# The last column of every scan: copied by ScalarE instead of VectorE

## The chip, the cores and the metric

The kernel runs on one core of a Trainium2 chip. The metric is the device time of one execution in microseconds (us). A core has five engines that run their own instruction streams in order and meet at semaphores: TensorE (PE, with its weight loads shown as PEld), VectorE (DVE), ScalarE (ACT), GpSimd (POOL) and SyncE (SP), which here mostly issues DMA transfers. SBUF is the on-chip working memory and PSUM the memory that PE writes; DRAM tiles lie in the chip's large memory.

## The reference

Two layers on an input `x` of 8 images of 64 x 64 pixels and 96 channels. The first is a selective scan over the pixels in four directions, the second a small network between an upsampling and a downsampling; each stands on a group normalisation and is added to its input. What the change touches is the scan:

```python
def step(h, inp):
    ul, dl, Bl, Cl = inp
    dA = jnp.exp(dl[..., None] * A)
    h = dA * h + (dl * ul)[..., None] * Bl[:, :, None, :]
    y = jnp.einsum('bkdn,bkn->bkd', h, Cl)
    return (h, y)
_, ys = lax.scan(step, h0, (u_t, d_t, B_t, C_t))
...
x = x + _L0_conv_ref(_gn(x), ...)
x = x + _L1_conv_ref(_gn(x), ...)
```

There are 4 directions (`k`), 192 channels (`d`), 16 states (`n`) and 4096 pixels, so for each image and direction 192 x 16 = 3072 independent recurrences of 4096 steps.

## The kernel before

**Tiles.** The work is cut into 3072 tiles of 128 partitions by 1024 pixels. A tile holds 8 channels with their 16 states, so 24 tiles (`NT`) cover the channels of one stretch of 1024 pixels, called a chunk here; 4 chunks (`NCH`) make one direction of one image, 4 directions an image, 8 images the whole: 128 chunks. The order is image, direction, chunk, tile. Since a tile sees only a quarter of the pixels, the state at its end must be kept until the tile of the same channels in the next chunk, 24 tiles later. It is kept in one column of `carry`, an SBUF tile of 128 x 24 with one column for each of the 24 tiles. In the first chunk of a direction the scan starts from 0.0, and after the last chunk nothing is kept.

**The steps of a tile.** `fetch` (L1059) has SP load `dub`, each channel's row repeated for 16 states. `product_b` (L1067) has GpSimd multiply it by `br` into `bb`. `decay` (L1071) has PE spread the step sizes into the PSUM tile `pd` (four matmuls, L1075), and ScalarE takes the exponential in place (L1082). `scan` (L1084) has VectorE run the recurrence (L1089). `product_c` (L1093) multiplies the states by `cr` into `hc` (L1095). `hold` (L1104) copies the last column of the scan into `carry` (L1108). `sums` (L1118) has PE add up the states of two tiles at a time (L1127), and `store` (L1157) sends the result to DRAM by way of ScalarE and SP.

**Two kinds of tiles.** Every third tile is marked `by_pool` (L1054). For it the scan writes to the SBUF tile `h`, GpSimd does `product_c`, and ScalarE does `hold`. For the other two of three the scan writes back into `pd`, VectorE does `product_c` straight after the scan, and VectorE does `hold` straight after that. Here these are called GpSimd tiles and VectorE tiles.

**Buffers.** `pd` has two buffers of two PSUM banks, so the matmul of tile i+2 may only write when all readers of tile i are done: the scan alone for a GpSimd tile, and the scan, the product and the copy for a VectorE tile. `bb`, `dub` and `hc` have four buffers, `h` two.

**The order.** The loop at L1193 writes out the order by hand. In step i, each engine's stream receives: the fetch of tile i+6 on SP, the product of the GpSimd tile i-1 and then `product_b` of tile i+3 on GpSimd, `decay` of tile i+1 on PE and ScalarE, then `scan`, `product_c` and `hold` of tile i. After that `side.advance` (L1250) adds pieces of all other work: normalisation, convolution and gates of the next image, the preparation of the next chunk (`prepare`, L965), the layer norm and the second network of the image before. A planner, `Side`, gives them out with fixed allowances for each engine and step (`CAPS`, L49). Then come `turn_over`, which puts in a matmul whose result nobody reads (L1101) where PE has little side work, and `sums` for tiles i-3 and i-2. The order is fixed when the program is built and does not react to what happens on the chip.

So the stream of ScalarE in step i is: exponential of tile i+1; the copy of `hold` if tile i is a GpSimd tile; side work. The stream of VectorE is: scan of tile i; if it is a VectorE tile, product and copy; side work.

Of the kernel before, what the change touches and what calls it, by code (L numbers as in the profile page):

```python
# [136 lines left out]
def kernel(ctx: ExitStack, tc: tile.TileContext, a: dict, out: bass.AP):  # L137
    nc = tc.nc
# [965 lines left out]
    def hold(t):  # L1104
        if t["last"]:
            return
        end = T - 1 if t["k"] < 2 else 0
        (nc.scalar.copy if t["by_pool"] else nc.vector.tensor_copy)(  # L1108
            carry[:, t["g"] : t["g"] + 1], t["h"][:, end : end + 1]
        )  # L1110

# [60 lines left out]
    with tc.manual_schedule():  # L1172
# [20 lines left out]
        for i in range(n + 4):  # L1193
            t = tiles[i] if i < n else None
# [48 lines left out]
            if t:  # L1243
                scan(t)
                if not t["by_pool"]:
                    product_c(t)
                hold(t)
# [105 lines left out]
```

## Time and profile before

| what | value |
|---|---|
| median of 3 runs | 11125.21 us (11121.33 to 11125.94) |
| the profiled execution's own time | 11107.68 us |
| its span, first to last instruction | 11105.8 us |
| mean clock granted to TensorE | 0.982 |
| scans (L1089) on VectorE | 3072, 2280 to 2350 ns each by form |
| products on VectorE (L1095) | 2048, 1225 ns each |
| copies of `hold` on VectorE | 1536, 148 ns each |
| copies of `hold` on ScalarE | 768, 183 ns each |
| `product_b` on GpSimd (L1069) | 3072, 2359 ns each |
| products on GpSimd (L1095) | 1024, 2357 ns each |
| exponentials on ScalarE (L1082) | 3072, 1088 ns each |
| bytes moved by DMA | 2401.27 MB, mean 216 GB/s |

The counts follow from the tiling: 3072 x 2/3 = 2048 products on VectorE, and three chunks of four keep their state, so 2048 x 3/4 = 1536 copies on VectorE and 1024 x 3/4 = 768 on ScalarE.

How to read the profile lines: a group of instructions has its line in the kernel, engine, operation, output and inputs by the program's names, shapes and count; then the time in which the group kept its engine busy, the mean duration of one in ns, and the idle time of the engine just ahead of such instructions with what ended most of it (`<-`). In a timeline the columns are the start in us from the beginning of the span, the duration in us, the engine, the line, and the instruction; idle time before it stands in brackets. Two instructions that follow one another on an engine can overlap by a few hundredths of a us in the records. The releaser named is inferred from semaphores and can be a neighbour of the true one.

### The profile page before, as it was taken

How to read it: one execution, taken by the hardware profiler on the slowest of the kernel's cores; microseconds unless marked ns; L12 is line 12 of the kernel's file. 1: busy time of each engine (PE TensorE's matmuls, PEld its weight loads, DVE VectorE, ACT ScalarE, POOL GpSimd, SP SyncE). 2: the span in 40 equal slices, each digit the busy share in tenths (PEclk: the TensorE clock that was granted, in tenths of full speed). 3: DMA queues.
4: the chain of work that ended last, by engine and by line, in shares of the span. 5: the costliest groups of instructions: out<-in, count | busy, mean ns of one | idle time of the engine just before them, and what ended most of it. 6: DMA issues, size and time to landing. Idle time of an engine off the chain costs nothing. (4 is left out here: it accounts for less than half of the span.)

```text
span 11105.8 us, 137238 instructions
## 1 busy us (share of the span) xinstructions
PE 9967.9 (90%) x45020; PEld 3204.6 (29%) x45020; DVE 10207.5 (92%) x7702; ACT 5910.6 (53%) x8218; POOL 10179.6 (92%) x4674
## 2 busy tenths in 40 slices
PE   8898888989889998999889998899988989889988
PEld 2222222322233222332223322233222332223325
DVE  6999999999999999999999999999999999999990
ACT  5455445656455564555545555455554655545543
POOL 5999999999999999999999999999999999999990
PEclk9999999999999999999999999999999999999998
DMA  6888898898988989888988989889898898988981
GB/s 174 215 208 224 209 231 209 217 227 232 233 209 216 225 231 225 212 218 224 240 217 215 224 221 244 209 219 225 217 243 210 217 228 218 247 206 216 227 214 48
DMA packets 1044463, 2401.27 MB, mean 216 GB/s; under 512 B 293820, under 2 KB 314556, under 8 KB 1043752
## 3 DMA queue, kind: packets, MB, share of 16 engines
q1 hardware_dynamic: 1042776, 2391.45, 86.5%
q8 instruction: 361, 5.91, 0.2%
q14 instruction: 350, 2.87, 0.1%
q10 hardware_dynamic: 976, 1.04, 0.0%
HBM read 1929.05 MB, written 328.73 MB: 203 GB/s over the span
## 5 line engine op out<-in xcount | busy, mean ns | idle before, releaser
L1069 POOL TENSOR_TENSOR bb<-dub,br 128x1024 f32<-128x1024 f32 x3072 | 7173.5, 2359 | 208.4 <-DMA dub<-du 149.2
L1082 ACT ACTIVATE pd<-pd,neg_a 128x1024 f32<-128x1024 f32 x3072 | 3340.7, 1088 | 4533.0 <-PE pd L1075 4489.8
L1075 PE MATMUL pd<-dl,sel_b 64*128 64x512 f32 x12288 | 3512.7, 645 | 987.2 <-DVE carry L1108 649.2
L1089 DVE TENSOR_TENSOR_SCAN pd<-pd,carry,bb 128x1024 f32<-128x1024 f32 x1536 | 3610.3, 2350 | 262.2 <-ACT carry L1108 127.9
L1095 POOL TENSOR_TENSOR hc<-h,cr 128x1024 f32<-128x1024 f32 x1024 | 2413.9, 2357 | 352.6 <-DVE h L1089 300.7
L1095 DVE TENSOR_TENSOR hc<-pd,cr 128x1024 f32<-128x1024 f32 x2048 | 2508.4, 1225 | 164.1 <-PE py L1127 20.0
L1075 PEld LDWEIGHTS pd<-dl,sel_b 64*128 64x128 f32 x12288 | 966.7, 186 | 3266.3 <-issue 1511.2
L1089 DVE TENSOR_TENSOR_SCAN h<-pd,carry,bb 128x1024 f32<-128x1024 f32 x768 | 1797.3, 2340 | 5.8 <-ACT pd L1082 5.6
L1127 PE MATMUL py<-hc,sel_r 128*32 128x512 f32 x12288 | 1715.0, 617 | 30.4 <-POOL hc L1095 30.2
L1089 DVE TENSOR_TENSOR_SCAN pd<-pd,bb 128x1024 f32<-128x1024 f32 x512 | 1172.5, 2290 | 98.6 <-ACT carry L1108 75.3
L1101 PE MATMUL idle<-sel_b,ident 128*128 128x512 f32 x1652 | 932.0, 646 | 8.0 <-DVE ty L720 5.9
L562 PE MATMUL pc<-pad,convr 96*128 96x512 f32 (+1 forms) x2304 | 858.3, 616 | 5.7 <-DVE e L585 3.6
L1089 DVE TENSOR_TENSOR_SCAN h<-pd,bb 128x1024 f32<-128x1024 f32 x256 | 583.6, 2280 | 26.0 <-ACT pd L1082 25.2
L1127 PEld LDWEIGHTS py<-hc,sel_r 128*32 128x32 f32 x12288 | 250.3, 109 | 1109.0 <-issue 854.5
L1031 POOL TENSOR_TENSOR u<-dl,u 128x512 f32<-128x512 f32 x384 | 485.0, 1271 | 79.2 <-DVE dl L1028 79.2
L862 PEld LDWEIGHTS p<-w2q,mq 128*100 128x100 f32 x4800 | 452.9, 168 | 274.6 <-issue 214.2
L855 PE MATMUL ph<-xu,w 96*128 96x500 f32 x960 | 504.9, 629 | 11.5 <-ACT mq L856 6.7
L862 PE MATMUL p<-w2q,mq 128*100 128x96 f32 x4800 | 511.5, 258 | 2.3 <-ACT mq L856 2.3
L562 PEld LDWEIGHTS pc<-pad,convr 96*128 96x128 f32 (+1 forms) x2304 | 266.3, 163 | 563.9 <-issue 552.8
L987 PE MATMUL px<-u,xp 64*64 64x512 f32 x1536 | 422.4, 627 | 2.4 <-issue 2.4
L1101 PEld LDWEIGHTS idle<-sel_b,ident 128*128 128x128 f32 x1652 | 249.8, 189 | 596.5 <-issue 522.4
L1012 PE MATMUL pv<-xd,dt_w 64*64 64x512 f32 x1536 | 394.4, 609 | 1.0 <-ACT xd L997 1.0
(153 smaller groups left out, 6707.9 us busy)
## 6 DMA issues: line engine op xcount, KB each, us to landing
dub<-du SPq DMA_DIRECT2D x3072, 512.0 KB
u<-u SPq DMA_DIRECT2D x256, 384.0 KB
du<-u SPq DMA_DIRECT2D x768, 128.0 KB
y<-yq SPq DMA_DIRECT2D x768, 128.0 KB
br<-xd SPq DMA_DIRECT2D x256, 256.0 KB
cr<-xd SPq DMA_DIRECT2D x256, 256.0 KB
yp<-y SPq DMA_DIRECT2D x384, 128.0 KB
yp<-u SPq DMA_DIRECT2D x192, 128.0 KB
```

The lines of the kernel that those rows point to most:

```text
L562: nc.tensor.matmul(t[rows].rearrange("p (i j) -> p i j", i=8), weights[:, cs], v["pad"][:, 8 * blk + kw : 8 * blk + kw + 8, kh : kh + H], ...
L855: nc.tensor.matmul(t[:, :px], w1[:, m, :], xu, start=True, stop=True)
L862: nc.tensor.matmul(t[:SIDE, C * i : C * i + C], sq[:, m, row], w2q[:, m, :], start=(m == 0), stop=(m == 2))
L987: nc.tensor.matmul(p[rows], xp[rows, k, q, :], v["u"][rows, q, :], start=(q == 0), stop=(q == 2), skip_group_check=True,)
L1031: nc.gpsimd.tensor_tensor(v["u"][:, q, :], got["dl"][:, q, :], v["u"][:, q, :], ALU.mult)
L1069: nc.gpsimd.tensor_tensor(t["bb"], t["dub"], t["got"]["br"], ALU.mult)
L1075: nc.tensor.matmul(pd[:, MB * hf : MB * hf + MB], sel_b[rows, 4 * t["s"] + t["j"]].rearrange("p n c -> p (n c)"), t["got"]["dl"][rows, t[" ...
L1082: nc.scalar.activation(pd, pd, AF.Exp, scale=neg_a[:, t["k"], t["g"] : t["g"] + 1])
L1089: nc.vector.tensor_tensor_scan(t["h"][:, ::step], pd[:, ::step], t["bb"][:, ::step], 0.0 if t["first"] else held, ALU.mult, ALU.add)
L1095: (nc.gpsimd if t["by_pool"] else nc.vector).tensor_tensor(t["hc"], t["h"], t["got"]["cr"], ALU.mult)
L1101: nc.tensor.matmul(p, ident, sel_b[:, 0:4].rearrange("p j n c -> p (j n c)"), start=True, stop=True)
L1127: nc.tensor.matmul(py[r0 : r0 + 32], sel_r[:, t["j"], :], t["hc"][:, MB * hf : MB * hf + MB], start=(t["j"] == 0), stop=(t["j"] == 3 and t ...
```

## The change

`hold` no longer chooses its engine by the kind of tile: ScalarE makes the copy for every tile. The copy of a VectorE tile so moves from VectorE's stream, where it stood behind the product, to ScalarE's, where it stands behind the exponential of tile i+1 and ahead of the side work of step i; it reads one column of `pd` in PSUM and writes one column of `carry` in SBUF, as before. Nothing else is edited.

```diff
     def hold(t):
         if t["last"]:
             return
         end = T - 1 if t["k"] < 2 else 0
-        (nc.scalar.copy if t["by_pool"] else nc.vector.tensor_copy)(
+        nc.scalar.copy(
             carry[:, t["g"] : t["g"] + 1], t["h"][:, end : end + 1]
         )
```

## The prediction

> **What bounds the kernel now.** I read the head of the page first, then the groups by line, then the timeline around the copies, then the busy time of chosen stretches.
>
> ```profile
> span 11105.8 us, 137238 instructions
> PE 9967.9 (90%) x45020; PEld 3204.6 (29%) x45020; DVE 10207.5 (92%) x7702; ACT 5910.6 (53%) x8218; POOL 10179.6 (92%) x4674
> ...
> L1082 ACT ACTIVATE pd<-pd,neg_a 128x1024 f32<-128x1024 f32 x3072 | 3340.7, 1088 | 4533.0 <-PE pd L1075 4489.8
> L1075 PE MATMUL pd<-dl,sel_b 64*128 64x512 f32 x12288 | 3512.7, 645 | 987.2 <-DVE carry L1108 649.2
> L1089 DVE TENSOR_TENSOR_SCAN pd<-pd,carry,bb 128x1024 f32<-128x1024 f32 x1536 | 3610.3, 2350 | 262.2 <-ACT carry L1108 127.9
> ```
>
> VectorE and GpSimd are both 92% busy, ScalarE 53%: the copy leaves the fullest engine for the emptiest. The first scan starts at 120.1 us and the last ends at 10836.3, so 10716 us belong to the 3072 tiles, 3.49 us each, and little else can change. Counted over the records of that stretch, VectorE is idle about 560 us and GpSimd about 570: neither is the bound everywhere, and what one gains the other must follow. ScalarE's 4533 us of idle time lie before the exponentials, waiting for the matmul that fills `pd`.
>
> Two views of the copies themselves, both from the listing by line:
>
> ```profile
> L1108 DVE COPY carry<-pd x1536: 146/148/151, 123.6 to 10750.5; 128x1 f32<-128x1 f32 x192
> L1108 ACT COPY carry<-h x768: 172/182/193, 133.1 to 10754.4; 128x1 f32<-128x1 f32 x192
> ```
>
> **The part removed.** 1536 copies at 148 ns would be 227 us, but that is not what VectorE loses. The timeline of VectorE in image 0 shows the same two tiles in a chunk with copies and, one chunk on, in the last chunk of a direction, where the kernel makes none:
>
> ```profile
> 1279.64 1.23 DVE L1095 TENSOR_TENSOR hc<-pd,cr 128x1024 f32<-128x1024 f32 x1
> 1280.78 0.15 DVE L1108 COPY carry<-pd 128x1 f32<-128x1 f32 x1
> 1280.85 2.35 DVE L1089 TENSOR_TENSOR_SCAN pd<-pd,carry,bb 128x1024 f32<-128x1024 f32 x1
> ...
> 1360.01 1.23 DVE L1095 TENSOR_TENSOR hc<-pd,cr 128x1024 f32<-128x1024 f32 x1
> 1361.15 2.35 DVE L1089 TENSOR_TENSOR_SCAN pd<-pd,carry,bb 128x1024 f32<-128x1024 f32 x1
> ```
>
> From the product's start to the next scan's start it is 1.21 us with the copy and 1.14 without: neighbours on VectorE overlap, and a copy costs 0.065 us (the median distance from copy to scan over some 1290 pairs). 1536 x 0.065 = 100 us, the most that VectorE alone can give.
>
> How much of it arrives is shown by whole chunks, since every fourth chunk already runs without these copies. Three chunks of image 0 with the same work in the background, then one from the next direction of a later image (columns: stretch, length, busy time of PE, weight loads, DVE, ACT, POOL, clock, DMA share, GB/s):
>
> ```profile
> 1196.83:1277.19 80.36, 67.57 (x264) 17.30 (x260) 77.25 (x59) 34.24 (x46) 77.79 (x36) 1.00 0.86 211
> 1277.19:1357.56 80.37, 67.57 (x264) 17.30 (x260) 77.26 (x60) 34.26 (x46) 77.83 (x36) 1.00 0.85 210
> 1357.56:1437.13 79.57, 67.57 (x264) 17.08 (x260) 76.21 (x43) 33.35 (x38) 77.78 (x36) 1.00 0.85 209
> 2870.66:2960.08 89.42, 78.39 (x335) 21.59 (x331) 83.51 (x71) 43.05 (x62) 87.29 (x43) 0.96 0.99 233
> ```
>
> VectorE's busy time falls by 1.05 us (16 x 0.065 = 1.04) and the chunk by 0.79 or 0.80. The quarter that is lost went into a longer wait of the scan that follows a GpSimd tile: there the product is not on VectorE, and the scan waits for the chain matmul, exponential of its own `pd`. So 0.79 us for each of the 96 chunks that make copies, 76 us, if all were like these. They are not: the last row is a stretch where the DMA share is 0.99 and GpSimd is busy 87.3 of 89.4 us, and VectorE has 6 us to spare. By records, 34 of the 96 chunks have a DMA share over 0.94 or less than 2 us of idle GpSimd. Their saving lies between 0 and 0.79; I take half, as some of these stretches still show waits for scans. Sum: 62 x 0.79 + 34 x 0.40 = 49.0 + 13.6 = 62.6 us.
>
> **The part added.** ScalarE gets 1536 copies. None in the trace reads one column of PSUM; the nearest rows are 182 ns (one column from SBUF, above) and 252 ns (the one-column activation from PSUM with a scale pointer, 96 partitions), 280 to 387 us in all. I take 0.2 us. This lies in the 4533 us that ScalarE idles before exponentials and costs nothing there: in the chunks above ScalarE is busy 34 of 80 us. Without that cover it would be 0.2 us a tile, 307 us.
>
> [...]
>
> **The waits that move.** (1) The copy must wait for the scan, and ScalarE runs in order, so all of ScalarE's work behind it waits too: the side work of that step and the exponential of tile i+2, and with them whoever needs their results, which are PE, VectorE and the stores that SP's queue sends. On ScalarE the copy of tile i stands just behind the exponential of tile i+1. Over the records this exponential ends 0.34 us (median) after scan i ends; in 19% of tiles it ends over 0.1 us before. The first side operation behind would start 0.17 us later on average, and the stretch from the last side operation to the next exponential is 0.98 us in the median, under 0.14 in a tenth. Cost 0 to 17 us; I take 5. (2) `pd` is now given back by the product on VectorE and by the copy on ScalarE, and the matmul of tile i+2 needs both. Placing the copy behind exponential and scan, it would end after the recorded start of that matmul in 19 of 1536 tiles, by 27 us in total, median margin 1.18 us before it. Cost 0 to 27; I take 5, as most of the 27 sits in a few long stalls. (3) The matmul no longer waits for the copy on VectorE (649.2 us of PE's waits name it): in tile triples without side work it starts 0.21 us after the product's end (median), and 0.05 to 0.15 in chunks without copies. Against this stands one more semaphore wait on PE, 51 ns where the trace has one. Taken as cancelling; between -36 us (512 tiles after a GpSimd tile, 0.07 more) and +36. (4) The next scan does not wait for the copy, although the page names it as the releaser: in this stretch of the timeline the scan starts when the exponential is over, before the copy is.
>
> ```profile
> 5016.13 1.09 ACT L1082 ACTIVATE pd<-pd,neg_a 128x1024 f32<-128x1024 f32 x1 [2.77 <-PE pd L1075]
> ...
> 5017.15 0.18 ACT L1108 COPY carry<-h 128x1 f32<-128x1 f32 x1
> ...
> 5017.32 2.36 DVE L1089 TENSOR_TENSOR_SCAN pd<-pd,carry,bb 128x1024 f32<-128x1024 f32 x1 [0.24 <-ACT carry L1108]
> ```
>
> [...]
>
> **Sum:** -62.6 + 5 + 5 = -53 us against the profiled execution's 11107.7, so 11055. The median of the runs shown, 11125.2, is 17.5 us above it; the same saving there gives 11072.
>
> **Rivals.** (a) No change: the freed time turns into other waits, chiefly of GpSimd and DMA. For it: GpSimd has only 566 us of idle time, and its work makes 78.7 us of a chunk (24 x 2.335 + 8 x 2.357 + 3 x 1.263), 0.9 under the fast one above. Against it: of its idle time 300.7 us is a wait for the scan, which gets shorter. If only one chunk in four keeps its 0.79, 19 us remain: 11106. (b) Slower: ScalarE's queue is blocked in wait (1), side results come late, PE (90% busy) stalls in order on them and the next `pd` is late. Price: 989 tiles with side work x 0.17 = 169 us if all of it reaches a scan, 11125 - 63 + 169 = 11231; it decides when more than 63 of the 169 arrive. Half of it gives 11147, the time I give this rival. For it: the tenth of tiles with under 0.14 us of room; against: the same copy already stands on ScalarE in 768 tiles. (c) More than forecast: triples of tiles without side work take 9.89 us with copies and 9.72 in the last chunks (medians), 0.17 us each; 768 triples make 131 us, 10994. For it: wait (3) is a real gain; against: the last chunks also lack ScalarE's copies, and crowded stretches can't give it. (d) The change doing something else than it says has no price of its own: a wait of the scan on the copy would be covered by the 1.14 us product in between.
>
> **How the numbers follow.** Forecast 0.58 (its own range is 62 x 0.79 - 27 = 22 us to 76 us saved, 11049 to 11103); (c) 0.14; (a) 0.15; (b) 0.13. A difference under 0.2% (22 us) can't be told from none here. Faster 0.58 + 0.14 = 0.72; same 0.15; slower 0.13. The range reaches from 11005, most of (c), to 11125, which takes in most of (a) and leaves out (b).
>
> **What would show it.** Right: VectorE's busy time down by about 100 us at the same counts, no copy between product and scan; ScalarE up by 120 to 310 us; GpSimd's wait for `h` under 300.7; chunks of image 0 near 79.6 us. Wrong: waits of scans for ScalarE growing above the present 348 us by more than 60, or PE waiting for ScalarE's copy in hundreds of tiles.

## The result and the profile after

The kernel became slower: 11189.36 us in the median (11178.06 to 11193.33, 4 runs) against 11123.27 before (11092.64 to 11125.94, 4 runs), a ratio of 1.0062 with a 95% interval of 1.005 to 1.0075. The prediction was 11072, faster, and its range ended at 11125.

The page after: the head and the groups that answer to those shown of before.

```profile
span 11190.4 us, 135908 instructions
PE 10007.9 (89%) x45020; PEld 3185.5 (28%) x45020; DVE 10122.3 (90%) x6166; ACT 6078.1 (54%) x9754; POOL 10189.0 (91%) x4674
...
L1082 ACT ACTIVATE pd<-pd,neg_a 128x1024 f32<-128x1024 f32 x3072 | 3339.2, 1087 | 3236.1 <-PE pd L1075 3225.2
L1075 PE MATMUL pd<-dl,sel_b 64*128 64x512 f32 x12288 | 3535.3, 650 | 1032.8 <-ACT carry L1108 700.1
L1089 DVE TENSOR_TENSOR_SCAN pd<-pd,carry,bb 128x1024 f32<-128x1024 f32 x1536 | 3611.2, 2351 | 388.5 <-ACT pd L1082 240.4
...
L1108 ACT COPY carry<-pd 128x1 f32<-128x1 f32 x1536 | 245.0, 160 | 1365.4 <-DVE hc L1095 1355.2
```

VectorE did get rid of its work: 10207.5 us busy became 10122.3, with 1536 instructions fewer. ScalarE grew by 168 us. The last group is the news. ScalarE stands idle for 1365 us ahead of its new copies, and what it waits for is not the scan (L1089) but the product (L1095). The idle time ahead of the exponentials shrank by nearly as much, 4533 to 3236 us, so on the totals alone this looks like a wait that has only changed its place. Counted over the records, VectorE's idle time between the first scan's start and the last one's end grew from 553 to 724 us, 171 us against the 86 of work that it saved there, and the stretch itself from 10716 to 10802.

The view by waits says who suffers (kernel after; total us, times, longest in us):

```profile
...
PEld pd L1075 <- ACT carry L1108: 1679.7, 1274, 7.2
...
PE pd L1075 <- ACT carry L1108: 700.1, 810, 6.3
...
DVE pd L1089 <- ACT pd L1082: 354.0, 569, 8.0
```

PE's matmuls into `pd` now wait for ScalarE's copy in hundreds of tiles; before, they waited 649.2 us for VectorE's copy. The last line is a scan that waits for its exponential; before, that line and the one that named ScalarE's copy had 113.8 and 203.2 us, now 354.0 and 50.2. With all forms of scans, the waits for ScalarE grew from 348 to 441 us.

The chunks of image 0 that the prediction leaned on (the same columns as there; two with copies, then the last chunk, without any):

```profile
1200.22:1281.75 81.53, 69.01 (x264) 17.16 (x260) 76.41 (x43) 36.50 (x62) 77.93 (x36) 0.98 0.85 209
1281.75:1363.24 81.49, 68.98 (x264) 17.08 (x260) 76.41 (x43) 36.52 (x62) 77.96 (x36) 0.98 0.85 207
1363.24:1442.40 79.16, 67.52 (x264) 17.08 (x260) 76.23 (x44) 33.37 (x38) 77.58 (x36) 1.00 0.85 209
```

VectorE's busy time in the first two is now that of a chunk without copies (76.4), as foreseen, and yet they take 81.5 us instead of 80.4. These rows do not show the cost of a wait alone, though: their clock column reads 0.98, and that of before reads 1.00. In the clock records each of the two has one stretch of 3.41 us in which TensorE was granted half of its clock, and the chunks of before have none. The first of them, in the same columns:

```profile
1226.32:1229.73 3.41, 3.41 (x12) 0.68 (x10) 3.38 (x4) 1.25 (x2) 3.41 (x3) 0.50 1.03 235
```

Up to this stretch the scans of the chunk lie within 0.13 us of their places in the chunk of before; behind it they are 0.9 us late or more. Over the whole execution half of the clock was granted for 484 us, against 396 before. That is a part of the loss, and the smaller one. A straight line through the 39 runs of the kernel before gives 6.5 us more for every 0.001 less of mean granted clock, and the four runs of the change have 0.0024 less: some 16 us, an estimate. And in the 47 chunks with copies in which neither execution has any half clock, the change takes 0.57 us more on average (95% interval 0.43 to 0.72), which would be 55 us in 96 chunks. Why less clock was granted is not shown.

The comparison chunk had no copies at all, on no engine; it showed what taking the copies away is worth and nothing of where they went.

### The profile page after: what moved, and what is told of

Same layout as the page of the kernel before. It is cut to its first block, busy times and chain, and to the rows that moved or that the text cites. A ratio compares the mean times of both kernels' runs of the same rounds, so it can differ in the third digit from the quotient of the medians.

```text
span 11190.4 us, 135908 instructions
## 1 busy us (share of the span) xinstructions
PE 10007.9 (89%) x45020; PEld 3185.5 (28%) x45020; DVE 10122.3 (90%) x6166; ACT 6078.1 (54%) x9754; POOL 10189.0 (91%) x4674
## 5 line engine op out<-in xcount | busy, mean ns | idle before, releaser
L1089 DVE TENSOR_TENSOR_SCAN pd<-pd,carry,bb 128x1024 f32<-128x1024 f32 x1536 | 3611.2, 2351 | 388.5 <-ACT pd L1082 240.4
L1095 POOL TENSOR_TENSOR hc<-h,cr 128x1024 f32<-128x1024 f32 x1024 | 2415.2, 2359 | 415.1 <-DVE h L1089 366.8
L1095 DVE TENSOR_TENSOR hc<-pd,cr 128x1024 f32<-128x1024 f32 x2048 | 2508.7, 1225 | 161.1 <-PE py L1127 19.3
L1089 DVE TENSOR_TENSOR_SCAN h<-pd,carry,bb 128x1024 f32<-128x1024 f32 x768 | 1798.0, 2341 | 8.9 <-ACT carry L1108 6.8
L1089 DVE TENSOR_TENSOR_SCAN pd<-pd,bb 128x1024 f32<-128x1024 f32 x512 | 1173.0, 2291 | 132.4 <-ACT pd L1082 113.5
L1108 ACT COPY carry<-pd 128x1 f32<-128x1 f32 x1536 | 245.0, 160 | 1365.4 <-DVE hc L1095 1355.2
L1089 DVE TENSOR_TENSOR_SCAN h<-pd,bb 128x1024 f32<-128x1024 f32 x256 | 583.9, 2281 | 35.2 <-ACT carry L1108 29.5
```

The lines of the kernel that those rows point to most:

```text
L1089: nc.vector.tensor_tensor_scan(t["h"][:, ::step], pd[:, ::step], t["bb"][:, ::step], 0.0 if t["first"] else held, ALU.mult, ALU.add)
L1095: (nc.gpsimd if t["by_pool"] else nc.vector).tensor_tensor(t["hc"], t["h"], t["got"]["cr"], ALU.mult)
```

## The experiments

Three kinds of tiles matter, so they get names: A is the first VectorE tile of every three (`i % 3 == 0`), B the second, P the GpSimd tile. In order the scans run A, B, P, A, B, P. After P the scan of the next A follows at once, as P's product is not on VectorE; that scan is the one that waits.

**Which half of the change loses.** Two kernels give ScalarE the copy of only A, or only B, besides those of P.

```diff
-        nc.scalar.copy(
+        (nc.scalar.copy if t["by_pool"] or t["i"] % 3 == 0 else nc.vector.tensor_copy)(
```

> ScalarE copies the last column for the GpSimd tiles and for the first VectorE tile of every three (i % 3 == 0), VectorE for the second (i % 3 == 1). Before is 11123, the change 11189: 100 us less on VectorE and 166 us more elsewhere. Chain theory (only the copy of the second VectorE tile lies on the chain product, copy, matmul, exponential to the scan that waits; the first one's buffer is needed 3.5 us later): 768 x 0.065 = 50 us gained and little lost, 11075 to 11095. Queue theory (ScalarE's stream stands still until the product is over, and all behind it comes late, whichever tile it is): half of both, -50 + 83, 11145 to 11165.

```diff
-        nc.scalar.copy(
+        (nc.scalar.copy if t["by_pool"] or t["i"] % 3 == 1 else nc.vector.tensor_copy)(
```

> The other half: ScalarE copies for the GpSimd tiles and for the second VectorE tile of every three, VectorE for the first. Chain theory: the whole loss of 166 us with half of the gain of 100, 11200 to 11240, slower than the full change. Queue theory: half of both, 11145 to 11165, as for the other half.

A alone: 0.999 (0.9981 to 0.9999), some 11 us gained. B alone: 1.0065 (1.0051 to 1.0079), 72 us lost, the whole of the loss, at nearly the granted clock of before (0.981 in the mean, 0.982 before). ScalarE stands in wait for products in both, 653.8 us in A alone and 806.0 in B alone. So it matters less that it stands in wait than where. A alone fell short of the 30 to 50 us that the chain theory gave it: of the 50 us of VectorE's time that it saves (768 x 0.065), 39 did not arrive as time.

**The wait by itself.** VectorE keeps all its copies; ScalarE additionally copies a column of the product into a scratch column, so it waits in the same place without holding `pd`.

```diff
+    sink = pp.tile([128, 1], F32, tag="sink", name="sink", bufs=1)
...
+        if not t["by_pool"]:
+            nc.scalar.copy(sink, t["hc"][:, end : end + 1])
```

> As before the change, VectorE makes its 1536 copies; ScalarE gets, at the place where the change puts the copy, a copy of one column of the product (SBUF) into a scratch column. So ScalarE waits for the product as in the change, but no PSUM buffer is held by it and VectorE keeps its work. Queue theory: the 166 us without the gain, 11250 to 11300. Chain theory: ScalarE is busy only half of the time and 1536 x 0.16 us go into its idle time, 11115 to 11150.

It came to 1.0069 (1.0057 to 1.0082), 76 us, between the two expectations: the wait alone costs something like the whole net loss, but less than half of what the queue theory had said. It stands for a slightly longer wait than the change has: this copy starts 0.09 us after the product's end (median) and takes 191 ns, where the copy of the change starts after 0.03 and takes 160. A second kernel keeps this extra copy for B only:

```diff
-        if not t["by_pool"]:
+        if t["i"] % 3 == 1:
             nc.scalar.copy(sink, t["hc"][:, end : end + 1])
```

> As wait_alone, but ScalarE's extra one-column copy of the product is there for the second VectorE tile of every three alone. The standing in wait cost 76 us for both tiles. If it costs wherever it stands (queue): half, ratio 1.002 to 1.0045. If it matters only where the next scan is already short of time (chain), all of it falls on this tile: 1.005 to 1.008. The rest of the 122 us that the copies of this tile cost in b_only (72 measured, 50 gained on VectorE) is then the late return of the PSUM buffer.

1.0063 (1.005 to 1.0076), 70 us (the copy starts 0.03 us after the product here). The cost falls on B, as the chain theory had it and against an even spread; the 6 us that would be left for A are inside the intervals.

Counted over the records of each kernel, for the scan of A behind P: how many of its exponentials stood ready and were held up over 0.06 us by ScalarE's other work, and the idle time of VectorE ahead of these scans (waits over 0.1 us, the first scan of the kernel left out).

| kernel | exponentials of A held up | waits of A's scans, us | ratio |
|---|---|---|---|
| before | 53 | 316 | 1 |
| A alone | 57 | 347 | 0.999 |
| B alone | 152 | 431 | 1.0065 |
| wait alone, both | 169 | 398 | 1.0069 |
| wait alone, B | 168 | 396 | 1.0063 |
| the change | 146 | 474 | 1.0062 |

The four kernels in which ScalarE waits for B's product, and only they, triple the number. Behind A's product ScalarE holds up just as much: where it waits for that (A alone, the wait for both, the change), 153 to 173 exponentials of P are held up, and 29 or 30 in the other three. But P's scan comes after B's product on VectorE, which gives its exponential that much more time: the waits of P's scans are 38 to 43 us there, 32 before. So the place in the pattern decides.

One such place of A, which comes back in seven of the eight images, first before and then after (timeline; some of ScalarE's and VectorE's lines):

```profile
1912.52 0.59 ACT L1160 COPY yq<-py 128x512 f32<-128x512 f32 x1
1912.56 1.22 DVE L1095 TENSOR_TENSOR hc<-pd,cr 128x1024 f32<-128x1024 f32 x1
1913.00 0.69 ACT L856 ACTIVATE mq<-ph,b 128x500 f32<-128x500 f32 x1
1913.57 0.77 ACT L849 ACTIVATE xu<-p,nb,rs 96x500 f32<-96x500 f32 x1
...
1915.09 1.09 ACT L1082 ACTIVATE pd<-pd,neg_a 128x1024 f32<-128x1024 f32 x1 [0.75 <-PE pd L1075]
...
1916.28 2.36 DVE L1089 TENSOR_TENSOR_SCAN pd<-pd,carry,bb 128x1024 f32<-128x1024 f32 x1 [0.16 <-ACT pd L1082]
```

```profile
1924.86 1.23 DVE L1095 TENSOR_TENSOR hc<-pd,cr 128x1024 f32<-128x1024 f32 x1
...
1926.00 2.34 DVE L1089 TENSOR_TENSOR_SCAN h<-pd,carry,bb 128x1024 f32<-128x1024 f32 x1
...
1926.11 0.16 ACT L1108 COPY carry<-pd 128x1 f32<-128x1 f32 x1 [1.06 <-DVE hc L1095]
1926.18 0.59 ACT L1160 COPY yq<-py 128x512 f32<-128x512 f32 x1
...
1926.66 0.68 ACT L856 ACTIVATE mq<-ph,b 128x500 f32<-128x500 f32 x1
1927.23 0.76 ACT L849 ACTIVATE xu<-p,nb,rs 96x500 f32<-96x500 f32 x1
...
1927.88 1.08 ACT L1082 ACTIVATE pd<-pd,neg_a 128x1024 f32<-128x1024 f32 x1
...
1929.06 2.36 DVE L1089 TENSOR_TENSOR_SCAN pd<-pd,carry,bb 128x1024 f32<-128x1024 f32 x1 [0.72 <-ACT pd L1082]
```

Before, the three side operations start while B's product runs or just after, and ScalarE then idles 0.75 us until the matmul is ready. After, they begin when the product is over, and the exponential, which has no idle time ahead of it any more, starts 3.02 us after the product's start instead of 2.53. The scan waits 0.72 us instead of 0.16.

**Why the copy waits for the product.** Product and copy only read `pd`; neither needs the other's result. If they are kept apart because both read `pd` in PSUM, the one that is written later must wait for the other, whichever that is. This kernel is the change with the copy ahead of the product:

```diff
                 scan(t)
+                hold(t)
                 if not t["by_pool"]:
                     product_c(t)
-                hold(t)
```

> The change with the copy placed ahead of the product of the same tile in the order written by hand. If the copy waits for the product because both read the same PSUM bank and are kept apart, the product must now wait for the copy: the exponential ahead of it on ScalarE ends 0.34 us (median) after the scan, the copy takes 0.16 to 0.2, so 1536 products start 0.3 to 0.6 us late, 11500 to 12000. If the wait has another reason (a count of semaphores that happens to cover the product), products and copies run side by side, the copy starts at the scan's end, and the time is 11050 to 11150.

1.0379 (1.0364 to 1.0393), 11529 us. Now the product waits for the copy, as VectorE's and ScalarE's lines of one tile show (the scan of this tile starts at 3001.99 and takes 2.36 us):

```profile
3003.80 1.11 ACT L1082 ACTIVATE pd<-pd,neg_a 128x1024 f32<-128x1024 f32 x1
3004.80 0.19 ACT L1108 COPY carry<-pd 128x1 f32<-128x1 f32 x1
3005.03 1.23 DVE L1095 TENSOR_TENSOR hc<-pd,cr 128x1024 f32<-128x1024 f32 x1 [0.68 <-ACT carry L1108]
```

Over the records, no product of these 1536 tiles starts less than 31 ns after the end of its copy. In the kernel after, no copy from `pd` starts less than 33 ns after the end of its product, in all 1536. The runs show the order being kept in both directions, by a wait that stands in the trace: VectorE is idle for 791.6 us ahead of products that wait for the copy here, ScalarE for 1355.2 us ahead of copies that wait for the product in the kernel after. What asks for this order is not shown, and what happens without it was not tried.

**The same change without a shared PSUM tile.** All scans go to the SBUF tile `h`, with three buffers; the room comes from small tiles elsewhere (those hunks are not shown). Once with VectorE's copies, once with ScalarE's.

```diff
-        t["h"] = sp.tile([128, T], F32, tag="h", name="h", bufs=2) if t["by_pool"] else pd
+        t["h"] = sp.tile([128, T], F32, tag="h", name="h", bufs=3)
```

> All scans go to the SBUF tile h with three buffers (room for it from one buffer less of the loaded sums and of the side work's e, and from the place of a weight that is used at the start only); product and copy as in the kernel before, the copy of VectorE tiles on VectorE. It stands beside the next run. The PSUM buffer is free when the scan ends: ratio 0.978 to 0.990 by the theory of the chain, 0.997 to 1.003 by its rival.

> The same with the change: ScalarE makes every copy, now from SBUF. Nothing of the copy shares a PSUM bank with the product, and no PSUM buffer waits for it. If the shared bank is what turned the change into a loss, ScalarE's copies start at the scan's end and the change is worth its 0.065 us a tile as far as GpSimd follows: 20 to 90 us less than the run before it in this list. If ScalarE's standing in wait is harmful in itself, 10 us or more above it.

Both are far slower than before, 1.1854 (1.1838 to 1.187) and 1.1757 (1.1741 to 1.1773); the last section shows which operations grew longer. What ends the waits of ScalarE's copies there is the scan, and nothing else is listed (total us, times):

```profile
  DVE h L1090: 2594.0, 1381
```

Of the 1536 copies of A and B, 1509 start before the product of their tile is over, half of them within 0.04 us of the scan's end. So two readers of one tile are not kept apart as such: of `h` in SBUF they are not, of `pd` in PSUM they are, in all 1536. Whether a bank is the unit there, or the tile of two banks, no run separates.

Between the two kernels ScalarE's copies save 108 us (13176.74 to 13068.31, intervals apart), near to 1536 x 0.065 = 100 and more than the 20 to 90 expected. The granted clock of the two differs (0.912 and 0.917 in the profiled executions), so a part of the 108 may be the clock. So where the copy shares no PSUM tile with the product, the change gains, by about what the prediction said it is worth on VectorE. The pair's products take 2447 ns instead of 1225, so this number does not carry over to it.

A third version, aimed at an earlier return of `pd`, scans into the buffer of the product and multiplies in place:

```diff
-        t["h"] = sp.tile([128, T], F32, tag="h", name="h", bufs=2) if t["by_pool"] else pd
+        t["h"] = sp.tile([128, T], F32, tag="h", name="h", bufs=2) if t["by_pool"] else sp.tile(
+            [128, T], F32, tag="hc", name="hc", bufs=4
+        )
...
-        t["hc"] = sp.tile([128, T], F32, tag="hc", name="hc", bufs=4)
+        t["hc"] = sp.tile([128, T], F32, tag="hc", name="hc", bufs=4) if t["by_pool"] else t["h"]
...
                 scan(t)
+                hold(t)
                 if not t["by_pool"]:
                     product_c(t)
-                hold(t)
```

> VectorE tiles scan into an SBUF buffer of the products (four buffers, as before), VectorE copies the last column, then multiplies in place; the PSUM buffer is free when the scan ends, 1.2 us earlier than before. Theory of the chain: most of the 251 us of waits of the scans behind GpSimd tiles goes, ratio 0.978 to 0.990, with GpSimd as the next bound. Rival (TensorE's side work sets those waits): 0.997 to 1.003. If the in-place product or its longer hold of a buffer costs VectorE or TensorE time: over 1.003.

1.278 (1.2763 to 1.2798). Its products are long too: 2776 ns.

**The copy behind ScalarE's side work.** If side work that is held up were all, moving the copy behind it should heal the change.

```diff
+            if t and not t["by_pool"]:
+                hold(t)
```

(after `side.advance`, with `hold` at its old place for P only)

> The change, with ScalarE's copy of a VectorE tile moved behind the side work of the same step, so that side work no longer stands behind the wait; the PSUM buffer still waits for the copy, and now for that side work too. If most of the loss is side work held up: 0.996 to 1.001. If it is the buffer that comes back late: 1.006 and more.

1.056 (1.0546 to 1.0574), nine times the loss of the change. The exponentials of A are held up by side work less than ever (19 times, 53 before), but `pd` comes back after that side work: the matmul starts 0.51 (A) and 0.54 us (B) after the product's end in the median, 0.21 before, and the waits of A's scans come to 833 us instead of 316. So the buffer must not return late either. Not all of it is that wait: half of the clock was granted for 847 us here, against 396.

**Versions that might win.** In the kernel before, VectorE's copy stands behind the product and is itself the last reader of `pd`. One kernel puts it ahead of the product, still on VectorE (an edit to the kernel before):

```diff
                 scan(t)
+                hold(t)
                 if not t["by_pool"]:
                     product_c(t)
-                hold(t)
```

> The kernel before, with one order changed: for a VectorE tile, VectorE makes the copy ahead of the product instead of behind it. No engine gets other work. Theory (the scan behind a GpSimd tile waits, 251 us in all, for a chain that starts when the last reader gives back the PSUM buffer of the second VectorE tile): the matmul can start 0.05 us after the product's end instead of 0.21, 480 waits x 0.16 = 75 us less, ratio 0.992 to 0.995. Rival (those scans wait because TensorE is busy with side work, whoever gives the buffer back): ratio 0.998 to 1.002.

0.9968 (0.9956 to 0.998), 35 us faster than before and the best of all runs. The gain is half of what was expected. The matmul does start 0.05 us after the product's end instead of 0.21 where it has nothing else to do, but the waits of A's scans fall only from 316 to 295 us; the idle time ahead of the products, 164.1 us before, fell to 56.0 as well. Two more keep the copy ahead of the product for B on VectorE and give A's copy to ScalarE, the first behind the product, the second behind the side work of the step (edits to the kernel before):

```diff
-        (nc.scalar.copy if t["by_pool"] else nc.vector.tensor_copy)(
+        (nc.vector.tensor_copy if t["i"] % 3 == 1 else nc.scalar.copy)(
...
                 scan(t)
+                if t["i"] % 3 == 1:
+                    hold(t)
                 if not t["by_pool"]:
                     product_c(t)
-                hold(t)
+                if t["i"] % 3 != 1:
+                    hold(t)
```

(the first; in the second, A's `hold` stands after `side.advance`)

> Made from the two halves that did not lose: for the second VectorE tile of every three VectorE copies ahead of the product (0.9968 for both tiles), for the first ScalarE copies behind it as in a_only (0.999). The gains add if they are of different links: 0.994 to 0.997. If the copy ahead of the product owes its gain to the first tile: 0.998 to 1.000.

> As mixed, with ScalarE's copy of the first VectorE tile behind the side work of its step. Its buffer is needed 3.5 us later at the earliest, so the lateness should be free and the side work is no longer held up: 10 to 40 us less than mixed. If the exponential that follows it on ScalarE is what suffers: same as mixed or slower.

0.9981 (0.9972 to 0.9991) and 1.0124 (1.011 to 1.0138). The first gained 20 us, less than the 0.994 to 0.997 expected if the gains add; what the earlier copy of B is worth by itself was not measured, so it stays open whether they do. In the second, A's buffer is not as patient as thought: the waits of P's scans, whose matmul needs that buffer, are 118 us, 54 in the first.

## Why the prediction was wrong

**The step that failed** is the first sentence on the waits that move: "The copy must wait for the scan". It waits for the product too, and started 1.35 us after the scan's end (median of the 1536). I had placed the copy behind the exponential of tile i+1 and the end of the scan, found it out of everybody's way in 1517 of 1536 tiles, and priced the block on ScalarE at 5 us and the buffer at 5. That ScalarE's read of `pd` would be kept behind VectorE's, as it is by 33 ns or more in all 1536 tiles, did not come into it. Every number of (1) and (2) was worked out from the wrong start: with the product's end in the place of the scan's, the same placing delays the first side operation behind by some 1.0 us on average, not by 0.17.

**The part removed** was right as work: VectorE's busy time fell by 85 us on the page (100 forecast), and in the pair without a shared PSUM tile the copies were worth 108, of which a part may be the clock. How much of the 62.6 us would have arrived without the new waits, no run shows by itself.

**The part added** was right in size: 160 ns a copy (0.2 taken), 168 us more for ScalarE, inside the 120 to 310 given.

**The wait on ScalarE (1)**, forecast at 0 to 17 us: 70 us for B, measured by itself, and for A nothing that the intervals tell from none. Its mechanism is the one of rival (b), the blocked queue, in a narrower place: the records show the side operations of B's step pushed in front of the exponential that A's scan waits for. PE's stalls on late side results, which (b) named, were not separated: PE's matmuls were held for them 31 us before and after, its weight loads 379 and 588. The rival's price, built on a delay of 0.17 us, was too small a delay on too many tiles.

**The buffer (2) and the wake of the matmul (3)**, forecast at 5 us and nil: not measured alone. If all of VectorE's 50 us would otherwise have arrived, B's copy on ScalarE costs 72 + 50 = 122 us, of which the wait explains up to 70; 52 are left, and most of A's 39. The records show what is in them: the matmul starts 0.245 us after the product's end instead of 0.21 (median, where it starts within 0.3 us of it), and the exponential 1.237 after the matmul's start instead of 1.168. That is 0.105 us later after the product's start, while VectorE is ready for the scan 0.065 earlier. With the wait for B alone both are as before, so that kernel does leave the buffer out. Why the exponential follows its matmul later is not shown; the one more semaphore wait on PE that (3) counted on is not in the trace, where separate waits ahead of these matmuls fell from 1520 to 837. The two costs are no clean sum: the wait for B alone held A's exponentials up by 130 us in all (37 before), B alone by 84, as `pd` itself is ready later there. So the split is an account from records, not an experiment; a kernel in which the buffer returns late and ScalarE doesn't wait could not be made, since both come from the same copy.

**The reading that the next scan does not wait for ScalarE's copy (4)** holds. In 1166 of the 1536 tiles the next scan starts before ScalarE's copy does, as P's does above (1926.00 and 1926.11). The extra copies on A leave the scans of B about where they were (88 waits over 0.1 us before, 104 with A alone).

**The signs given for being wrong** both appeared: waits of scans for ScalarE up by 93 us (60 was the mark), and PE waiting for ScalarE's copy in hundreds of tiles. Two signs of being right failed to appear: GpSimd's wait for the scan grew from 300.7 to 366.8 us, and the chunks of image 0 took 81.5 us, not 79.6. Rival (b) had 13% and the right side.

## What to carry to other kernels

Before moving a small operation to an idle engine, list what it will be ordered against there, other readers of the same PSUM tile included; here a copy of one column, 160 ns long, waited for a product of 1.23 us with which it shares only the PSUM tile it reads. Idle time of an engine is cover only if the wait ends before the next thing behind it is due: price each place in the pattern by itself, since here the wait for one of two like products cost nothing measurable and the wait for the other about 70 us. A stretch without the operation shows what removing it is worth, not what moving it is worth. And two stretches are alike only if their clock column is: half of TensorE's clock for 3.41 us made some 0.9 of the 1.17 us by which the first chunk shown here is longer than before.

## What the runs showed of the hardware that was not expected

With both inputs of VectorE's product in SBUF, that product and `product_b` on GpSimd both took longer. In the version with all scans in SBUF and VectorE's copies, the product takes 2447 ns in the mean (1225 with one input in PSUM), `product_b` on GpSimd 2900 (2359 before), while scans, with one input in PSUM, take 2332 (2340 and 2350 before; groups by line, the line numbers are one higher here):

```profile
L1070 POOL TENSOR_TENSOR bb<-dub,br 128x1024 f32<-128x1024 f32 x3072 | 8847.3, 2900 | 136.7 <-DVE h L1090 123.1 <-DMA dub<-du 6.9
L1090 DVE TENSOR_TENSOR_SCAN h<-pd,carry,bb 128x1024 f32<-128x1024 f32 x2304 | 5336.3, 2332 | 55.1 <-ACT carry L1109 30.6 <-ACT pd L1083 23.3
L1096 DVE TENSOR_TENSOR hc<-h,cr 128x1024 f32<-128x1024 f32 x2048 | 5012.4, 2447 | 146.2 <-PE py L1128 5.0 <-DVE h L1090 2.3 <-issue 0.4
```

One such meeting in its timeline:

```profile
1506.35 5.64 POOL L1070 TENSOR_TENSOR bb<-dub,br 128x1024 f32<-128x1024 f32 x2
1506.58 3.19 DVE L1096 TENSOR_TENSOR hc<-h,cr 128x1024 f32<-128x1024 f32 x1
```

The product starts while GpSimd is inside an operation and takes 3.19 us instead of 1.23. The 1802 products of this run that start inside a GpSimd operation end 1.08 us (median) after that operation does, a little less than the 1.23 us of a product, as if they did their work behind it. That they wait for GpSimd is an inference from these times; what the two share is not shown. In the kernel before, 1980 of the 2048 products start inside a GpSimd operation, and all 2048 take 1.22 to 1.23 us. In this kernel, scanning in place in PSUM is therefore not only a saving of room: VectorE's products from `pd` keep their time beside GpSimd's operations, and those from `h` did not. The three versions that left it are 18 to 28% slower. In the one that scans into the products' buffer, VectorE's products took 3176 us more and the kernel 3093; the granted clock fell too, to 0.888, and in the pair some buffers are fewer, so not all of the 18 to 28% need be this.
